# Reordering the first DMAs, table loads and a silu at the start of a 32-batch mixture-of-experts kernel

## The chip, the cores and the metric

The kernel runs on one core of a Trainium2 chip (trn2). The metric is the device time of one execution in microseconds. Beside it stands one profiled execution, whose trace gives every instruction on the engines TensorE (PE; its weight loads are PEld), VectorE (DVE), ScalarE (ACT), GpSimd (POOL) and SyncE (SP), and the packets of the DMA queues.

## The reference

The input x is 32 batches of 128 tokens by 128 features, fp32; cond is 32 by 128. Two layers follow each other, each "x plus a feed-forward of a conditioned mixture of experts". Only the front of the first layer matters here:

```
x = x + _L0_ffn_ref(_L0_cond_ref(x, cond_1024, ...), ...)
x = x + _L1_ffn_ref(_L1_cond_ref(x, cond_1024, ...), ...)

# in _L0_cond_ref
gate_logits = concat(means of three token groups) @ gate_w + gate_b
mod = silu(time_cond) @ time_w + time_b              # silu of cond
gate_logits = gate_logits * (1 + scale) + shift      # scale, shift: halves of mod
top 2 of softmax(gate_logits) weigh 4 experts per batch
out    = sum over experts of weight * mask * (gelu(x @ ew1 + eb1) @ ew2 + eb2)
shared = gelu(x @ sw1 + sb1) @ sw2 + sb2             # all tokens
return out + shared
```

Gelu is the tanh approximation. Inputs and weights are read from HBM by DMA.

## The kernel before, in words

Features lie on the 128 partitions and tokens along the free axis. The 4096 tokens are cut into 8 blocks of 512 (4 batches each): xT[0] to xT[7]. The first layer's shared expert works block by block. `shared_up` (L274 on) issues four matmuls (L279) of a block against the four 128-column chunks of `sw1_t`, each into a PSUM bank of its own, and for each a gelu on ScalarE with a bias from `par` (L280) into `hs`. `shared_down` (L286 on) adds the four second matmuls (L290, weights `sw2_t`) into one bank; VectorE writes the result to `c0all` (L294). In the profile the weights sw1_t and sw2_t are both called sw_t.

Blocks 0 to 4 are done first, then the routed experts: 36 units of one expert and up to two batches each, for which SP fetches weights by an index that the kernel computes itself; then blocks 5 to 7; then the feed-forward that takes most of the time (L253, L750), and the second layer. The function `pipelined` (L217) runs each unit's up part ahead of the previous unit's down part. So TensorE's order at the front is up 0, up 1, down 0, up 2, down 1, up 3, down 2 and so on. Matmul results take PSUM banks in rotation: six banks for `mm_tile`, two for `y_tile`; a matmul into a bank that was used before waits until its earlier reader is done.

Into this stream a table `between` (L639) hooks other work at named points, such as `("up", "s", 2, 2)`, in front of block 2's third up matmul: `cond_gates` (L301). It contains three small matmuls for the gate logits (L310), one of silu(cond) with time_w (L314), one of cond with the second layer's router weights (L316, read by VectorE into `tsb` at L317, which L433 multiplies into `diag`), and then a chain on VectorE with one exp on ScalarE (L327), giving the gate weights `gl` and the chosen experts `maskc`. `schedule` follows in front of block 3 (its small matmuls L356 and L357 need `maskc`), and `spread_slots` in front of block 4.

The order of instructions on each engine is made by the framework's scheduler from data dependences, except where `tc.keep_in_program_order(...)` pins an instruction to its place in the program. A scalar activation whose function isn't in the table that is loaded gets an ACT_TABLE_LOAD in front of it. Before the change nothing at the front is pinned on ScalarE: its silu of cond (L229), gelus and exp lie where the scheduler put them.

The first DMAs are issued on two queues, SP's and ScalarE's (L154 to L177):

```
    nc.scalar.dma_start(out=sw1_t[:, :P], in_=sw1[:, :P])         # L156
    nc.sync.dma_start(out=xT[0][:, half], in_=x[0][:, half])      # L157
    half = slice(TB // 2, TB)
    nc.scalar.dma_start(out=xT[0][:, half], in_=x[0][:, half])    # L159
    nc.sync.dma_start(out=sw1_t[:, rest_w], in_=sw1[:, rest_w])   # L160
    nc.scalar.dma_start(out=par, in_=packed)                      # L161
```

Sizes: 64 KB (L156), 128 KB each half of x[0], 192 KB (L160), and `par`, 411 columns of small parameters on 128 partitions, 205 KB. The first four columns of `par` are the shared expert's first biases, sb1. After these SP issues x[1] (L162), sw2 (L163), x[2] to x[7] (L165) and the big weights. Completions are counted on eight semaphores in rotation, so a DMA's issue can wait for the one that used its semaphore before.

`tiny` is a 1x1 tile that the second layer uses to ask for a table ahead of time (`table`, L877 on).

Of the kernel before, what the change touches and what calls it, by code (L numbers as in the profile page):

```python
# [34 lines left out]
AF = mybir.ActivationFunctionType  # L35
# [6 lines left out]
TB = BB * S  # L42
# [41 lines left out]
def columns(cols):  # L84
    out, at = {}, 0
    for name, n in cols:
        out[name] = slice(at, at + n)
        at += n
    return out, at


AT, NCOLS = columns(COLS)
# [6 lines left out]
def adaln_ffn(  # L99
# [3 lines left out]
    nc = tc.nc  # L103
# [14 lines left out]
    def mm_tile(name):  # L118
        taken["mm"] += 1
        return banks[:, (taken["mm"] - 1) % NM, :]  # L120
# [13 lines left out]
    def const(shape, name, dtype=F32):  # L134
        return cpool.tile(shape, dtype, tag=name, name=name)


    par = const([P, NCOLS], "par")
    par32 = const([P, NCOLS32], "par32")
    rows = const([P, NROW], "rows")  # L140
    sw1_t = wpool.tile([P, H], F32, tag="sw1", name="sw1_t")
# [8 lines left out]
    xT = [xall[:, b * TB : (b + 1) * TB] for b in range(NB)]  # L150
# [4 lines left out]
    half, rest_w = slice(0, TB // 2), slice(P, H)  # L155
    nc.scalar.dma_start(out=sw1_t[:, :P], in_=sw1[:, :P])  # L156
    nc.sync.dma_start(out=xT[0][:, half], in_=x[0][:, half])  # L157
    half = slice(TB // 2, TB)
    nc.scalar.dma_start(out=xT[0][:, half], in_=x[0][:, half])  # L159
    nc.sync.dma_start(out=sw1_t[:, rest_w], in_=sw1[:, rest_w])  # L160
    nc.scalar.dma_start(out=par, in_=packed)  # L161
    nc.sync.dma_start(out=xT[1], in_=x[1])  # L162
    nc.sync.dma_start(out=sw2_t, in_=sw2.rearrange("(c p) d -> p c d", p=P))  # L163
    for blk in range(2, NB):
# [14 lines left out]
    def col(name, i=0, n=1):  # L179
        return par[:, AT[name].start + i : AT[name].start + i + n]  # L180


    ones = const([B, P], "ones")
    nc.gpsimd.memset(ones, 1.0)
    tri = const([P, E1, E1], "tri")
    nc.gpsimd.memset(tri, 0.0)
    for e in range(1, E1):
# [38 lines left out]

    cT = par[:, AT["cond"]]
    sT = const([P, B], "sT")
    nc.scalar.activation(sT, cT, AF.Silu)  # L229
    full, hp, wp, head, prop, wrist = (const([P, B], n) for n in ("full", "hp", "wp", "hd", "pr", "wr"))  # L230

    def sums(blk):
        xb = batches(xT[blk])
        at = slice(blk * BB, (blk + 1) * BB)
        lo = 0
        for to, n in ((head, NHEAD), (prop, NPROP), (wrist, NHEAD)):
            V.tensor_reduce(to[:, at], xb[:, :, lo : lo + n], AX.X, ALU.add)
            lo += n
# [5 lines left out]
    def before(*point):  # L244
        for do in between.pop(point, ()):
            do()
# [27 lines left out]
    def shared_up(blk):  # L274
        h = work.tile([P, NC, TB], F32, tag="h", name=f"hs0_{blk}", bufs=3)
        ps = [mm_tile(f"us_{blk}_{c}") for c in range(NC)]
        for c in range(NC):
            before("up", "s", blk, c)
            nc.tensor.matmul(ps[c], lhsT=sw1_t[:, c * P : (c + 1) * P], rhs=xT[blk], start=True, stop=True)  # L279
            nc.scalar.activation(h[:, c, :], ps[c], AF.Gelu_apprx_tanh, bias=col("sb1", c))  # L280
        if blk < 2:
            for b in range(4 * blk, 4 * blk + 4):
                sums(b)
        return h
# [350 lines left out]
    def first_rows():  # L635
        gates_to_dram("f", 0)
        fgates[0] = fetch_rows(0)

    between.update({  # L639
        ("up", "s", 2, 2): [cond_gates],  # L640
        ("up", "s", 3, 0): [schedule],
        ("up", "s", 4, 0): [spread_slots],
# [8 lines left out]
    nc.gpsimd.memset(c0all[:, FIRST * TB :], 0.0)  # L651
    nc.gpsimd.memset(xall[:, NB * TB :], 0.0)
    L0 = {"s": (shared_up, shared_down), "p": (unit_up, unit_down)}
    units = [("s", b) for b in range(FIRST)] + [("p", q) for q in UNITS]
    units += [("s", b) for b in range(FIRST, NB)]
# [214 lines left out]
    def in_order(inst):  # L870


        tc.keep_in_program_order(inst)

    tiny = const([1, 1], "tiny")

    def table(func):  # L877

# [18 lines left out]
    def sh_up(group, k, of=None, h=None, later=None):  # L897

        e, c = divmod(k, 2)
        if h is None:  # L900
            h = work.tile([P, SB, TB], F32, tag="h", name=f"hs_{group}_{k}", bufs=3)
        for at, b in enumerate(blocks(group)):
            if of in (None, at):
                g, u = mm_tile(f"g1_{b}_{k}"), mm_tile(f"u1_{b}_{k}")
                by_columns(g, sws_t[0][:, e, c, :], x1T[b], 32)
                by_columns(u, sws_t[1][:, e, c, :], x1T[b], 32)


                def finish(g=g, u=u, at=at, b=b):
                    table(AF.Silu)  # L910
                    in_order(glu(g, u, h[:, at, :], f"s1_{b}_{k}"))

                finish() if later is None else later.append(finish)
        return h
# [162 lines left out]
    h = STAGES["f"][0](*units[0][1:])  # L1077
    for unit, after in zip(units, units[1:]):
# [3 lines left out]
        h = ahead  # L1082
# [4 lines left out]
    for group in (1, 2):  # L1087
# [49 lines left out]
        if group == 1:  # L1137
            h = sh_up(2, 0)
# [123 lines left out]
```

## Time and profile before

| what | value |
|---|---|
| time, median of 3 runs | 966.85 us (966.79 to 967.62) |
| the profiled execution: time, span | 966.89 us, 965.1 us |
| TensorE clock in the records (mean) | 1.00 |
| first matmul (L279), ended by the DMA of x | 4.54 us |
| silu of cond (L229), ended by the DMA of par | 7.38 us |
| first gelu (L280) | 8.92 us, 0.69 us long |
| tables loaded on ScalarE up to 24 us | 4, of 1.28 us each |
| exp of the gate (L327) | 22.27 us |
| first matmul of a routed expert (L521) | 41.73 us |
| DMA share and rate, 2.0 to 4.5 us | 0.92, 255 GB/s |

The span runs from the first to the last instruction; the profiled execution's own time is 1.8 us longer. In the timeline a row merges equal instructions that follow each other: start, length, engine, line, operation, written tile <- read tiles, partitions x elements, count, and in brackets the idle time before it and what ended it. An fp32 matmul call is two MATMUL rows (two passes), each with a weight load. A matmul's end is modelled and overlaps the next one's start, so the rate is read from starts.

### The profile page before, as it was taken

The numbers are of one execution on the slowest core, as the hardware profiler recorded it, in microseconds if no ns is written. First come the engines' busy times: TensorE is split into PE (matmuls) and PEld (weight loads), VectorE is DVE, ScalarE is ACT, GpSimd is POOL, SyncE is SP. The second block draws the span as 40 slices with busy tenths as digits, with TensorE's granted clock in tenths as the row PEclk, the third lists the DMA queues.
The fourth block names the chain that finished last, engine by engine and source line by source line (L and its number), as shares of the span: only waits on it lengthen the run. The fifth ranks groups of instructions, "written<-read, shape, count | busy, mean of one in ns | idle before, by whom it ended". The sixth has DMA issues, their size and how long they took to land.

```text
span 965.1 us, 15705 instructions
## 1 busy us (share of the span) xinstructions
PE 951.8 (99%) x6138; PEld 444.3 (46%) x6138; DVE 593.5 (61%) x1118; ACT 351.7 (36%) x622; POOL 75.1 (8%) x86
## 2 busy tenths in 40 slices
PE   8999999999999999999999999999999999999997
PEld 3588984444444444444444444444444443322333
DVE  4444574766866776686676887668667655633323
ACT  5355544223322322232232332223223223456674
POOL 0000001200101011010101011011010000000000
PEclk9999999999999999999999999999999999999999
DMA  9745641000000000000000000000000003040101
GB/s 315 245 143 171 213 138 48 2 1 4 1 1 2 1 1 1 1 1 1 2 2 1 1 2 3 1 2 1 1 1 1 1 1 89 1 91 1 45 2 45
DMA packets 22850, 38.13 MB, mean 40 GB/s; under 512 B 1968, under 2 KB 13232, under 8 KB 22768
## 3 DMA queue, kind: packets, MB, share of 16 engines
q1 hardware_dynamic: 22192, 36.48, 12.4%
q8 instruction: 53, 0.87, 0.4%
q10 hardware_dynamic: 576, 0.54, 0.2%
q14 instruction: 29, 0.24, 0.1%
HBM read 34.65 MB, written 2.36 MB: 38 GB/s over the span
## 4 chain that ended last, share of the span: by engine, by line
PE 84%; ACT 1%; DVE 0%; issue 0%; DVEq 0%; ACTq 0%
PE banks L253 57%; PE banks L750 20%; PE banks L890 3%; PE banks L290 1%; PE banks L984 1%; ACT hl L992 0%; PE banks L279 0%; PE banks L553 0%; PE banks L266 0%; PE banks L568 0%; PE banks L582 0%; DVE pg L978 0%; DVE pT L979 0%; ACT hs L280 0%; DVE fin L1176 0%
## 5 line engine op out<-in xcount | busy, mean ns | idle before, releaser
L667 ACT ACTIVATE sf<-banks 128x512 f32<-128x512 f32 x256 | 152.7, 597 | 435.3 <-PE banks L253 421.4
L668 DVE TENSOR_TENSOR hf<-sf,banks 128x512 f32<-128x512 f32 x256 | 174.8, 686 | 183.0 <-PE banks L253 182.2
L253 PE MATMUL banks<-c0all,wg_t 128*64 128x512 f32 x1024 | 263.5, 593 | 0.0
L253 PE MATMUL banks<-cg,wu_t 128*64 128x512 f32 x1024 | 263.1, 592 | 0.0
L253 PEld LDWEIGHTS banks<-cg,wu_t 128*64 128x64 f32 x1024 | 73.4, 137 | 146.3 <-issue 126.9
L253 PEld LDWEIGHTS banks<-c0all,wg_t 128*64 128x64 f32 x1024 | 72.8, 137 | 121.4 <-issue 108.8
L662 POOL PARTITION_BROADCAST fg<-fgT x64 | 72.7, 1149 | 655.1 <-DVE cg L711 493.6
L750 PE MATMUL banks<-t,wd_t 128*64 128x256 f32 x512 | 121.0, 379 | 0.0
L750 PE MATMUL banks<-hf,wd_t 128*64 128x256 f32 x512 | 104.2, 379 | 0.0
L750 PEld LDWEIGHTS banks<-hf,wd_t 128*64 128x64 f32 x512 | 53.4, 137 | 55.4 <-issue 36.8
L750 PEld LDWEIGHTS banks<-t,wd_t 128*64 128x64 f32 x512 | 70.1, 137 | 0.0
L524 ACT ACTIVATE h<-banks,w 128x256 f32<-128x256 f32 (+3 forms) x136 | 49.6, 433 | 49.4 <-PE banks L521 49.3
L750 PE MATMUL banks<-hf,a_sum 128*64 128x256 f32 x512 | 66.1, 379 | 0.0
L750 PE MATMUL banks<-t,a_sum 128*64 128x256 f32 x256 | 65.7, 379 | 0.0
L730 DVE TENSOR_TENSOR hf<-hf 128x512 f32<-128x512 f32 x64 | 63.0, 984 | 2.2
L253 PE MATMUL banks<-xall,rw_t 128*32 128x512 f32 x512 | 58.4, 593 | 0.2 <-ACT hl L992 0.2
L253 PE MATMUL banks<-xall,sws 128*32 128x512 f32 x512 | 57.4, 593 | 0.2 <-ACT hl L992 0.2
L537 PE MATMUL banks<-h,w 128*128 128x256 f32 (+3 forms) x272 | 52.5, 338 | 0.0
L521 PE MATMUL banks<-x,w 128*128 128x256 f32 (+3 forms) x272 | 52.2, 337 | 0.0
L521 PEld LDWEIGHTS banks<-x,w 128*128 128x128 f32 x272 | 45.3, 190 | 4.4 <-issue 1.0
L537 PEld LDWEIGHTS banks<-h,w 128*128 128x128 f32 x272 | 44.7, 190 | 4.1 <-issue 0.7
L965 ACT ACTIVATE hr<-banks 128x512 f32<-128x512 f32 x64 | 36.9, 591 | 25.6 <-PE banks L253 25.4
(211 smaller groups left out, 775.1 us busy)
## 6 DMA issues: line engine op xcount, KB each, us to landing
w<-in_experts SPq DMA_DIRECT2D x36, 514.5 KB
wg_t<-in_w_gate SPq DMA_DIRECT2D x8, 256.0 KB
wu_t<-in_w_up SPq DMA_DIRECT2D x8, 256.0 KB
wd_t<-in_w_down SPq DMA_DIRECT2D x8, 256.0 KB
gates<-rg SPq DMA_DIRECT2D x4, 512.0 KB
gates<-rg SPq DMA_DIRECT2D x8, 256.0 KB
xall<-in_x SPq DMA_DIRECT2D x7, 256.0 KB
out<-fin SPq DMA_DIRECT2D x6, 256.0 KB
```

Source lines behind the costliest of these rows:

```text
L253: mm = nc.tensor.matmul(ps[own, :], lhsT=w[:, own], rhs=x, start=True, stop=True)
L290: nc.tensor.matmul(y, lhsT=sw2_t[:, c, :], rhs=h[:, c, :], start=(c == 0), stop=(c == NC - 1))
L521: nc.tensor.matmul(ps[c][:, :m, :n], lhsT=w1, rhs=x[:, :m, :n], start=True, stop=True)
L524: nc.scalar.activation(h[:, c, :m, :n], ps[c][:, :m, :n], AF.Gelu_apprx_tanh, bias=bias)
L537: nc.tensor.matmul(y[:, :m, :n], lhsT=w2, rhs=h[:, c, :m, :n], start=(c == 0), stop=(c == NC - 1))
L662: nc.gpsimd.partition_broadcast(bc, row)
L667: silu = nc.scalar.activation(s, ps_gate, AF.Silu)
L668: V.tensor_tensor(h, s, ps_up, ALU.mult)
L730: V.tensor_tensor(b12, b12, b11, ALU.subtract)
L750: nc.tensor.matmul(y[half, n], lhsT=w[:, c, :], rhs=h[:, c, :], start=first, stop=(e == EF - 1 and last))
L890: in_order(nc.tensor.matmul(y[32 * j : 32 * (j + 1)], lhsT=w, rhs=h, start=first, stop=last))
L965: in_order(nc.scalar.activation(h[:, at, :], ps, AF.Gelu))
```

## The change

It does four things at the front. The DMA of the small parameters is split: the four bias columns go second on ScalarE's queue, the other 407 columns fourth. The second half of x[0] goes on SP's queue instead of ScalarE's, and the rest of sw1 on ScalarE's instead of SP's. A 1x1 gelu on `tiny` (allocated earlier, behind `ones`) stands in front of all other activations and is pinned, as are the gelus of blocks 0 and 1. And the silu of cond is hooked in front of the first matmul of down 0, which by the program's order is behind block 1's gelus, and pinned there.

```diff
     half, rest_w = slice(0, TB // 2), slice(P, H)
     nc.scalar.dma_start(out=sw1_t[:, :P], in_=sw1[:, :P])
     nc.sync.dma_start(out=xT[0][:, half], in_=x[0][:, half])
-    half = slice(TB // 2, TB)
-    nc.scalar.dma_start(out=xT[0][:, half], in_=x[0][:, half])
-    nc.sync.dma_start(out=sw1_t[:, rest_w], in_=sw1[:, rest_w])
-    nc.scalar.dma_start(out=par, in_=packed)
+    half, biases = slice(TB // 2, TB), AT["sb1"].stop
+    nc.scalar.dma_start(out=par[:, :biases], in_=packed[:, :biases])
+    nc.sync.dma_start(out=xT[0][:, half], in_=x[0][:, half])
+    nc.scalar.dma_start(out=sw1_t[:, rest_w], in_=sw1[:, rest_w])
+    nc.scalar.dma_start(out=par[:, biases:], in_=packed[:, biases:])
     nc.sync.dma_start(out=xT[1], in_=x[1])
...
     nc.gpsimd.memset(ones, 1.0)
+
+    tiny = const([1, 1], "tiny")
+    tc.keep_in_program_order(nc.scalar.activation(tiny, ones[:1, :1], AF.Gelu_apprx_tanh))
...
     sT = const([P, B], "sT")
-    nc.scalar.activation(sT, cT, AF.Silu)
...
-            nc.scalar.activation(h[:, c, :], ps[c], AF.Gelu_apprx_tanh, bias=col("sb1", c))
+            gelu = nc.scalar.activation(h[:, c, :], ps[c], AF.Gelu_apprx_tanh, bias=col("sb1", c))
+            if blk < 2:
+                tc.keep_in_program_order(gelu)
...
     between.update({
+        ("down", "s", 0, 0): [lambda: tc.keep_in_program_order(nc.scalar.activation(sT, cT, AF.Silu))],
         ("up", "s", 2, 2): [cond_gates],
...
-
-    tiny = const([1, 1], "tiny")
```

The built program after the change, engine by engine, has ScalarE do: gelu table, 1x1 gelu, 8 gelus, silu table, silu, gelu table, 2 gelus of block 2, exp table, exp, gelu table, 2 gelus of block 2, then as before. Before: silu table, silu, gelu table, 11 gelus, exp table, exp, gelu table, 1 gelu. On TensorE the matmul of L316 moves behind block 2's third and fourth up matmuls, and of block 4's four down matmuls one instead of two stands in front of the first routed unit. On VectorE the copy of `tsb` and the product `diag` move behind the subtraction that feeds exp (L326). SP has the same number of DMAs, the third x block's now with a wait for an earlier DMA.

## The prediction

> **What bounds the kernel now.** I read the page first, then the timeline of TensorE and of its weight loads from 0 to 46 us, then ScalarE's over the same stretch, then the DMA queues of the microseconds before the first matmul. The page:
>
> ```profile
> span 965.1 us, 15705 instructions
> ...
> PE 951.8 (99%) x6138; PEld 444.3 (46%) x6138; DVE 593.5 (61%) x1118; ACT 351.7 (36%) x622; POOL 75.1 (8%) x86
> ```
>
> TensorE's share is 99%, but a busy PE need not be a PE at its peak, so the start is looked at closely. Its timeline (start, length, engine, line, operation, operands, count; each fp32 matmul call is two passes):
>
> ```profile
> 4.54 9.07 PE L279 MATMUL banks<-xall,sw_t 128*128 128x512 f32 x16 [4.54 <-DMA xall<-in_x]
> 13.45 3.60 PE L290 MATMUL banks<-hs,sw_t 128*128 128x512 f32 x8
> 16.89 1.88 PE L279 MATMUL banks<-xall,sw_t 128*128 128x512 f32 x4
> 18.70 0.23 PE L310 MATMUL banks<-par,full 128*32 128x4 f32 x2
> ...
> 18.91 0.21 PE L314 MATMUL banks<-par,sT 128*32 128x8 f32 x2
> 18.97 0.21 PE L316 MATMUL banks<-par 128*32 128x8 f32 x2
> 19.11 1.98 PE L279 MATMUL banks<-xall,sw_t 128*128 128x512 f32 x4
> 20.93 3.60 PE L290 MATMUL banks<-hs,sw_t 128*128 128x512 f32 x8
> ```
>
> The reader is to see that the only idle time is the 4.54 us in front, and that a DMA of the input x ends it. From then on each row begins where the one before lets it: 8 passes in 3.44 us (13.45 to 16.89) is 0.429 us a pass, and the same 0.429 holds whether gelus are late or early. Up to 136 us TensorE has no idle gap. The weight loads show the rate of the first passes:
>
> ```profile
> 5.53 0.34 PEld L279 LDWEIGHTS banks<-xall,sw_t 128*128 128x128 f32 x1 [0.52 <-issue]
> 6.38 0.34 PEld L279 LDWEIGHTS banks<-xall,sw_t 128*128 128x128 f32 x1 [0.52 <-issue]
> 7.23 0.34 PEld L279 LDWEIGHTS banks<-xall,sw_t 128*128 128x128 f32 x1 [0.52 <-issue]
> 8.09 0.34 PEld L279 LDWEIGHTS banks<-xall,sw_t 128*128 128x128 f32 x1 [0.52 <-issue]
> 8.73 0.19 PEld L279 LDWEIGHTS banks<-xall,sw_t 128*128 128x128 f32 x1 [0.31 <-issue]
> 9.16 0.19 PEld L279 LDWEIGHTS banks<-xall,sw_t 128*128 128x128 f32 x1 [0.24 <-issue]
> ```
>
> They come 0.85 us apart until 8.09 and 0.43 apart from 8.73: TensorE runs at half rate for some 4 us (to about 8.5), though the clock row says 1.00. ScalarE:
>
> ```profile
> 2.13 1.28 ACT L229 ACT_TABLE_LOAD   x1 [2.13 <-issue]
> 7.38 0.23 ACT L229 ACTIVATE sT<-par 128x32 f32<-128x32 f32 x1 [3.97 <-DMA par<-in_packed]
> 7.63 1.28 ACT L280 ACT_TABLE_LOAD   x1
> 8.92 3.70 ACT L280 ACTIVATE hs<-banks,par 128x512 f32<-128x512 f32 x6
> ...
> 17.94 0.69 ACT L280 ACTIVATE hs<-banks,par 128x512 f32<-128x512 f32 x1 [3.60 <-PE banks L279]
> ...
> 20.98 1.28 ACT L327 ACT_TABLE_LOAD   x1
> 22.27 0.20 ACT L327 ACTIVATE gl<-gl 32x4 f32<-32x4 f32 x1
> 22.49 1.28 ACT L280 ACT_TABLE_LOAD   x1
> ```
>
> The first gelu starts at 8.92, although its matmul ended near 6.6: ScalarE waited for all of par (silu at 7.38), then loaded gelu's table. That looks like 2.3 us to win, but nobody waits for them. The first matmul that needs a bank back is call 7, at 11.73; it wants the first gelu, over at 9.61: 2.1 us to spare. The second GEMM starts at 13.45, when block 0's four gelus have been over since 11.3. ScalarE then idles 3.60 us before 17.94. So in this stage TensorE's own issue sets the end, behind the arrival of its first operands.
>
> **The change, part by part.** *Gelu's table first, biases in a DMA of their own.* ScalarE now issues four DMAs at 0.45 us each (0.73 to 2.55), loads the table (to 3.85), and does the 1x1 activation. Its first gelu can start when call 1 ends. Gain on the path: 0, since TensorE fills the 2.1 us of slack already; the gelus just wait for matmuls. The biases are 128 rows of 16 B; the trace's 80-byte packets (rows) take 12 ns, so they cost some 0.1 us of an engine's time and should land by about 3.5, against a need near 5.8. If they came 2 us later, that slack would still cover them.
>
> *Order of the first DMAs.* This is the part that lies on the path, because the start of TensorE is set by the second half of x[0]. Before, that half went second on ScalarE's queue, beside the 192 KB rest of sw1 on SP's. The packets of the trace: the second half 2.81 to 4.04, its completion 4.40; the sw1 rest 2.54 to 3.88, its completion 4.22; first matmul 4.54. The queues from 2.5 to 4.05 us (packets, MB, share of 16 engines):
>
> ```profile
> q1 hardware_dynamic: 207, 0.27, 62.9%
> q10 hardware_dynamic: 235, 0.18, 41.2%
> ```
>
> Both queues are served side by side, SP's (q1) getting more bytes. After the change the half of x goes second on SP's queue and takes the place that the sw1 rest had there (packets from 2.54); beside it run the tail of sw1's first quarter, the biases, and only then the sw1 rest, third on ScalarE's queue, issued 0.46 us later than before. Upper bound of the gain: the half alone, 0.13 MB at the 0.29 MB/us of this window, ends at 2.54 + 0.45 = 2.99, so 1.05 us sooner; sw1's first quarter, whose completion came at 3.29, limits that to 1.1 as well. Lower bound: 0, if the sw1 rest takes the same share as before. Nearest row: the sw1 rest itself in that place, 192 KB against a competitor, in 1.34 us; 128 KB at its rate is 0.89 us, which ends at 3.43, 0.6 sooner; since its competitor is nearly empty at first I take 0.65. First matmul at 3.9.
>
> Does the sw1 rest become late? It is wanted two passes later, 3.9 + 1.84 = 5.74. Nearest row: its own transfer before, 1.68 us from first packet to completion; from about 2.9 that gives 4.6. The other end: third on ScalarE's queue before was par, of the same size, 3.69 to 7.36; that span from 2.9 gives 6.6 and a stall of 0.8. I take 4.6, since the traffic beside it is the x half and x[1], not par's neighbour with its many 512-byte packets. Cost 0.
>
> x[1] and sw2 keep their places in SP's queue (wanted at 9.4 and 12.8, completed at 7.18 and 7.89). The third block's DMA, which went out at 2.58, now waits for the first quarter of sw1 (3.3); two 256 KB transfers stand queued ahead of it, so nothing runs dry. What SP issues behind it is unchanged, and w of the first pair landed at 37.3, used at 41.7.
>
> *Silu behind the second block's gelus.* It now costs two table loads more on ScalarE there (silu, and gelu again), and the stage has five loads instead of four. They stand in order before block 2's gelus, the exp and block 3's. From the rows: the last gelu of block 1 ends at 14.34; 1.28 + 0.23 + 1.28 and some 0.05 between give 17.2, and the next gelu's matmul is ready at 17.94. Covered by the 3.60 us of idle time, 0.75 left; without cover it would cost up to 2.8. The Trainium skill speaks against this step: "ScalarE: Activation LUTs", section "What ACT_TABLE_LOAD costs", charges every switch a drain beside the load, about 2.66 us in all, and its rules say to batch by table set. With it silu would last until 19.9, and the exp likewise (below). The trace shows 1.28 us, next instruction 0.01 to 0.02 us later: exp's excursion takes 20.96 to 23.79, which is 2 x 1.28 + 0.20 + 0.06. The row decides; cost 0.
>
> *What the scheduler moved with it.* The built order differs in three places. Exp is now asked for after two of block 2's gelus instead of three: table by 20.8, its input (VectorE's chain, without the tsb copy and diag product) by 20.4, so it runs 1.5 us earlier, and the last two gelus end at 23.6 instead of 24.5. The tsb copy now stands in front of the softmax sum and waits for its matmul, about 21.2; the sum still comes 0.7 us sooner than its 22.51. And the matmul of L316 (cond by r1t) leaves the group of five small ones and stands alone behind block 2's last up matmul. Small matmuls have a fixed price per group: five take 18.17 to 19.64 where two large passes would take 0.86, so 0.61; two (L356, L357) take 23.93 to 25.20, so 0.41. That is 0.07 a call and 0.28 a group. One group more: +0.27, on the path. The later regrouping of block 4's second GEMM around the first expert pair moves no total.
>
> Sum: -0.65 + 0.27 = -0.38. The profiled execution took 966.89 (1.8 around its span); the median shown is 966.85. So 966.5.
>
> **The rivals.**
> *Nothing gained in front.* The sw1 rest takes its share all the same and the start stays at 4.54: 966.85 + 0.27 = 967.1. Or the start moves but the half rate ends at the same instant, 8.5. The Trainium skill, "TensorE: Matmul & The Clock Gate", Part 1, has the gate judge a free-running window, so the half-rate stretch need not begin with the kernel. The trace shows one such stretch, 4.0 us. If it moves along, 0.65 counts in full; if it ends where it ended, 0.33: 966.8. Being free-running, on average over launches it counts in full, which is what I use. For this rival: both queues share the engines, so what one gains the other takes. Against it: the x half gets a place in which packets began at 2.54 instead of 2.81, and meets less beside it.
>
> *Slower: the second piece of weights is late.* Third on ScalarE's queue, the sw1 rest lands at 6.6 as par's row would have it. From 5.74 on TensorE stands still, 0.8 us, and the quiet pushes the end of half rate back by a window (3.4 us in the same section of the skill, half of it lost, 1.7). -0.38 + 0.8 + 1.7 = +2.1: 969.0. It decides from a landing after about 5.7. Against it: the piece's own 1.68 us.
>
> *The drain is real on a switch from silu.* First gelu of block 2 at 19.9, exp over at 24.0, its mask at 25.8 where L356 would want it at 24.7 (stall 1.05), and bank 4 free at 27.4 where block 3's second matmul comes at 26.95 (0.45): 966.5 + 1.5 = 968.0.
>
> *Half rate shorter.* The window falls well and half rate ends one half to one window sooner than its 4 us: a further 0.9 to 1.7, so 964.8 to 965.6.
>
> **How the numbers follow.** Forecast 0.58 (966.5, its own range 966.0 to 967.0); nothing gained 0.22 (966.8 to 967.1); late weights 0.07 (969.0); drain 0.05 (968.0); shorter half rate 0.08. The range 965.6 to 967.9 covers the first two and takes in the three shown runs' spread of 0.8; it leaves out late weights and nearly all of the last two, 0.2 at most. About 0.2%, 1.9 us, is what a measurement of this kernel can tell from no change: faster (under 964.9) is most of the last case, 0.05; slower (over 968.8) is late weights, 0.07; the rest 0.88.
>
> **What would show it.** In the changed profile: the first L279 matmul near 3.9 instead of 4.54; weight loads 0.85 apart for about 4 us, no gap between the second and third; first gelu near 5.8 instead of 8.92; silu's excursion inside 14 to 17.3 with a wait for TensorE before the next gelu; a lone small matmul with about 0.28 around it near 21; everything after 25 us shifted by one constant, about -0.4. I am wrong if TensorE shows an idle gap between its second pass and 25 us, if the start stays above 4.3, or if the shift is not constant after 46 us.

## The result and the profile after

The changed kernel takes 969.1 us (median of 22 runs, 967.95 to 969.95), beside 967.37 us for the kernel before in 22 runs (966.28 to 968.33). The ratio is 1.0017, 95% interval 1.0011 to 1.0023: slower by about 1.7 us. The forecast of 966.5 and its range up to 967.9 missed it. The time is close to that of the rival with the late second piece of weights (969.0), in part by luck: the rival was worked out as +2.1 from a before of 966.85, the median of three runs, where 22 runs give 967.37 and a shift of +1.7. The profiled execution took 969.95, its span is 968.2. It is one of the slowest of its 22, and the profile before (966.89) is 0.5 under its median, so the shift between the two profiles (+3.1) is larger than that of the medians (+1.7).

The page after, as before (busy time, share, instructions):

```profile
span 968.2 us, 15710 instructions
...
PE 954.4 (99%) x6138; PEld 445.2 (46%) x6138; DVE 593.5 (61%) x1118; ACT 353.7 (37%) x624; POOL 75.1 (8%) x86
```

TensorE has the same 6138 instructions and still 99%, and is busy 2.6 us longer. So most of what the profile lost hides inside "busy". The timeline of TensorE at the front (line numbers are three to five higher than before: L282 is the up matmul, L295 the down matmul, L321 the lone small one):

```profile
3.76 2.04 PE L282 MATMUL banks<-xall,sw_t 128*128 128x512 f32 x2 [3.76 <-DMA xall<-in_x]
7.12 9.11 PE L282 MATMUL banks<-xall,sw_t 128*128 128x512 f32 x14 [1.31 <-DMA sw_t<-in_sw]
16.07 3.60 PE L295 MATMUL banks<-hs,sw_t 128*128 128x512 f32 x8
19.50 1.88 PE L282 MATMUL banks<-xall,sw_t 128*128 128x512 f32 x4
...
21.66 1.98 PE L282 MATMUL banks<-xall,sw_t 128*128 128x512 f32 x4
23.57 0.23 PE L321 MATMUL banks<-par 128*32 128x8 f32 x2
23.73 3.70 PE L295 MATMUL banks<-hs,sw_t 128*128 128x512 f32 x8
```

The start came 0.78 us sooner (3.76 for 4.54). But the row of 16 passes is cut behind the second: 1.31 us of idle time, ended by a DMA of sw_t, the rest of sw1. By the distance of 1.84 us between the first and third passes of before, the third was due at 5.60; it came 1.52 later (more than the idle time, as the end of a pass is modelled). The weight loads show the second loss:

```profile
3.73 0.50 PEld L282 LDWEIGHTS banks<-xall,sw_t 128*128 128x128 f32 x2 [3.73 <-DMA sw_t<-in_sw]
7.12 0.50 PEld L282 LDWEIGHTS banks<-xall,sw_t 128*128 128x128 f32 x2 [2.88 <-DMA sw_t<-in_sw]
8.13 0.34 PEld L282 LDWEIGHTS banks<-xall,sw_t 128*128 128x128 f32 x1 [0.52 <-issue]
...
12.40 0.34 PEld L282 LDWEIGHTS banks<-xall,sw_t 128*128 128x128 f32 x1 [0.52 <-issue]
13.06 0.19 PEld L282 LDWEIGHTS banks<-xall,sw_t 128*128 128x128 f32 x1 [0.33 <-issue]
13.49 0.19 PEld L282 LDWEIGHTS banks<-xall,sw_t 128*128 128x128 f32 x1 [0.24 <-issue]
```

Loads stay 0.85 us apart until 12.40, where before they were 0.43 apart from 8.73. The trace's record of the granted clock says the same: full from 8.51 before, from 12.86 after. Laid against the passes of before, the shift is -0.78 at the start, +0.74 at the third pass, +2.6 at the tenth, +2.9 behind the lone L321, and +3.1 at the end. In this execution: -0.78 (start) + 1.52 (stall) + 1.87 (longer half rate) + 0.30 (L321) = +2.91. From 46 us on the shift is not quite the one constant that was forecast: it stays at 2.91 to 118 us, grows there by 0.16 and at 167 us by 0.04, and then stays at 3.11. What adds these 0.2 is open.

ScalarE went as forecast, moved along by TensorE's delay:

```profile
2.61 1.28 ACT L188 ACT_TABLE_LOAD   x1 [2.61 <-issue]
3.90 0.20 ACT L188 ACTIVATE tiny<-ones 1x1 f32<-1x1 f32 x1
5.84 0.69 ACT L283 ACTIVATE hs<-banks,par 128x512 f32<-128x512 f32 x1 [1.74 <-PE banks L282]
...
16.97 1.28 ACT L645 ACT_TABLE_LOAD   x1
18.27 0.23 ACT L645 ACTIVATE sT<-par 128x32 f32<-128x32 f32 x1
18.51 1.28 ACT L283 ACT_TABLE_LOAD   x1
20.56 0.69 ACT L283 ACTIVATE hs<-banks,par 128x512 f32<-128x512 f32 x1 [0.76 <-PE banks L282]
```

The first gelu starts 3.08 us sooner than before, and behind the silu's two loads ScalarE still idles 0.76 us until its matmul is there.

Where the piece of weights was: the queues from 3.25 to 4.25 us, SP's (q1) and ScalarE's (q10), as packets, MB and share of the 16 engines. Of before:

```profile
q1 hardware_dynamic: 98, 0.14, 58.5%
q10 hardware_dynamic: 133, 0.13, 52.3%
```

Of after:

```profile
q1 hardware_dynamic: 46, 0.09, 53.9%
q10 hardware_dynamic: 61, 0.06, 17.4%
```

The engines moved 0.15 MB there instead of 0.27. The rest of sw1 had its first packet at 3.25 and completed at 7.07; x[1], third on SP's queue, completed at 6.89. Before, the two second-place transfers had completed at 4.22 and 4.40, and the third-place ones at 7.18 (x[1]) and 7.36 (par).

### The profile page after: what moved, and what is told of

It reads as the page before. It is cut to its first block, busy times and chain, and to the rows that moved or that the text cites. A ratio compares the mean times of both kernels' runs of the same rounds, so it can differ in the third digit from the quotient of the medians.

```text
span 968.2 us, 15710 instructions
## 1 busy us (share of the span) xinstructions
PE 954.4 (99%) x6138; PEld 445.2 (46%) x6138; DVE 593.5 (61%) x1118; ACT 353.7 (37%) x624; POOL 75.1 (8%) x86
## 4 chain that ended last, share of the span: by engine, by line
PE 83%; ACT 1%; DVE 0%; issue 0%; DVEq 0%; ACTq 0%
PE banks L256 57%; PE banks L756 20%; PE banks L894 3%; PE banks L295 1%; PE banks L988 1%; ACT hl L996 0%; PE banks L282 0%; PE banks L558 0%; PE banks L269 0%; PE banks L573 0%; PE banks L587 0%; DVE pg L982 0%; DVE pT L983 0%; ACT hs L283 0%; DVE fin L1180 0%
```

## The experiments

The theory (late by its place): what goes third on ScalarE's queue shares the engines with x[1], third on SP's, and lands near 7 as par did before; TensorE stops behind its second pass, and the stop prolongs the half rate. The rivals: the loss is elsewhere, in the silu with its two table loads or in the small matmul ("elsewhere"); the stop counts with its length only, and doesn't prolong the half rate ("stop alone"); and later, the 16-byte rows of the biases clog the queues ("small rows"). Ratios are to the kernel before on the same chip, with 95% intervals. The cuts of the edits show the lines that are new; of the lines that they replace, some are left out.

**One part alone.** Into the kernel before goes only the order of the DMAs (e4), and into it only the swap of the two second transfers, without the biases (e1):

```diff
 # e4_dma_part: before, with
+    half, biases = slice(TB // 2, TB), AT["sb1"].stop
+    nc.scalar.dma_start(out=par[:, :biases], in_=packed[:, :biases])
+    nc.sync.dma_start(out=xT[0][:, half], in_=x[0][:, half])
+    nc.scalar.dma_start(out=sw1_t[:, rest_w], in_=sw1[:, rest_w])
+    nc.scalar.dma_start(out=par[:, biases:], in_=packed[:, biases:])
 # e1_swap_only: before, with
+    nc.sync.dma_start(out=xT[0][:, half], in_=x[0][:, half])
+    nc.scalar.dma_start(out=sw1_t[:, rest_w], in_=sw1[:, rest_w])
+    nc.scalar.dma_start(out=par, in_=packed)
```

> The kernel before with the DMA part of the change alone (biases second, rest of sw1 third, other parameters fourth on ScalarE's queue; x half second on SP's); silu and the tables where they were before. Late-weights theory: start near 3.8, a gap of about 1.3 us before the third pass, half rate until one window later in most runs: the whole loss less the lone small matmul, 969.1 - 0.3 = 968.8. Rival, ScalarE's order: back to 967.4 or below.

> The kernel before, with one exchange: the second half of x[0] second on SP's queue, the rest of sw1 second on ScalarE's; par whole and third, silu and tables as before. Late-weights theory (what hurts is the third place on ScalarE's queue): here the rest of sw1 is second and runs beside the x half, lands by about 4.4, TensorE starts at about 4.2 and has no gap before its third pass; time 967.4 - 0.3 = 967.1. Rival, the queue itself (ScalarE's queue loses against SP's wherever the piece stands): the piece lands after 5.9, a gap of about 1 us as in the changed kernel, time near 969. Rival, ScalarE's new order: no difference to before at all, 967.4.

e4: 968.69 us, 1.0015 (1.0008 to 1.0021). The order of the DMAs alone makes nearly the whole loss. What is missing (0.2 us by the two ratios, less than their intervals can tell) fits the 0.3 of the lone small matmul, which e4 doesn't have. "Elsewhere" falls. Its TensorE:

```profile
3.79 2.04 PE L280 MATMUL banks<-xall,sw_t 128*128 128x512 f32 x2 [3.79 <-DMA xall<-in_x]
6.88 2.93 PE L280 MATMUL banks<-xall,sw_t 128*128 128x512 f32 x3 [1.05 <-DMA sw_t<-in_sw]
```

The same early start and nearly the same stop, with silu and gelus where they were. e1: 966.9 us, 0.9998 (0.9989 to 1.0006). With the piece second on ScalarE's queue it lands at 4.39 and there is no stop; the start is 4.29, 0.25 sooner (TensorE up to 9 us):

```profile
4.29 5.46 PE L279 MATMUL banks<-xall,sw_t 128*128 128x512 f32 x6 [4.29 <-DMA xall<-in_x]
```

The swap of the two queues is harmless; what hurts is that the biases stand in front of the piece.

**The change with the piece in time.** Both are the changed kernel with the biases third on ScalarE's queue: e3 with the piece second there and the x half on SP's queue, e2 with both on the queues of before.

```diff
 # e3_biases_third: after, with
-    nc.scalar.dma_start(out=par[:, :biases], in_=packed[:, :biases])
     nc.sync.dma_start(out=xT[0][:, half], in_=x[0][:, half])
     nc.scalar.dma_start(out=sw1_t[:, rest_w], in_=sw1[:, rest_w])
+    nc.scalar.dma_start(out=par[:, :biases], in_=packed[:, :biases])
 # e2_old_places: after, with
+    nc.scalar.dma_start(out=xT[0][:, half], in_=x[0][:, half])
+    nc.sync.dma_start(out=sw1_t[:, rest_w], in_=sw1[:, rest_w])
+    nc.scalar.dma_start(out=par[:, :biases], in_=packed[:, :biases])
```

> The changed kernel with two DMAs of ScalarE's queue exchanged: the rest of sw1 second, the biases third. Late-weights theory: start near 4.2, rest of sw1 landed by 4.5, no gap, 967.4 - 0.3 + 0.3 = 967.4; the first gelu is not later than its matmul, since biases land by about 5. Rival, the queue itself: the gap of about 1.3 us stays, 969. Rival, the small DMA: the gap stays, since the 16-byte rows are still there.

> The changed kernel, with the second half of x[0] and the rest of sw1 on the queues of before; the biases third on ScalarE's queue, the other parameters fourth; gelu table first and silu moved as in the change. Late-weights theory: start at 4.5, no gap behind the second pass, half rate over about 4 us after the start, and what is left of the change is one small matmul that stands alone, +0.3: 967.7. Rival, ScalarE's order (silu and its two table loads cost TensorE something): stays near 969. Rival, the small DMA of 16-byte rows: a stall remains too, at least 968.5.

e3: 966.97 us, 0.9999 (0.9991 to 1.0008); start 4.08, no stop (up to 9 us):

```profile
4.08 5.42 PE L282 MATMUL banks<-xall,sw_t 128*128 128x512 f32 x6 [4.08 <-DMA xall<-in_x]
```

e3 and the changed kernel differ only in the order of the piece and the biases, and their intervals do not meet: this exchange alone takes the loss away. e2: 967.71 us, 1.0004 (0.9995 to 1.0012); start 4.45, no stop. In e2 everything of the change but the order of the DMAs is left. Its lone small matmul stands between large ones:

```profile
19.71 1.99 PE L282 MATMUL banks<-xall,sw_t 128*128 128x512 f32 x4
21.63 0.23 PE L321 MATMUL banks<-par 128*32 128x8 f32 x2
21.79 3.70 PE L295 MATMUL banks<-hs,sw_t 128*128 128x512 f32 x8
```

From 19.71 to 21.79 is 2.08 us for four large passes and the small call, against the 1.72 of four passes at 0.43; what the small call would have cost inside its group, 0.07, leaves 0.29. The shift against before grows by 0.29 at this place in e2 and by 0.30 in e3. In these traces it is the only price that the silu, the gelus and the scheduler's moves put on the path; the time of e2 fits it, but its interval holds no change as well.

**The stop filled.** The first up matmul is done twice (the second writes the same values), so that TensorE has work where it stood still:

```diff
 # e5_filled: after, with
+            for _ in range(2 if blk == 0 and c == 0 else 1):
                 nc.tensor.matmul(ps[c], lhsT=sw1_t[:, c * P : (c + 1) * P], rhs=xT[blk], start=True, stop=True)
```

> The changed kernel, in which TensorE does the very first matmul call twice (the same result into the same bank), so that it works through most of its gap. Theory with two terms (the gap of 1.3 us, and the half rate that lasts longer because TensorE stood still): the second call takes 1.7 us at half rate, the third pass pair starts 0.3 us later than in the changed kernel, but half rate ends at the first boundary after some 4 to 7 us of work instead of starting its count again after the gap: in the trace half rate over by about 10.5 at the latest; time 0.5 to 1.0 us below the changed kernel's 969.1, so 968.3. Rival, only waiting costs and the half-rate stretch is what it is: 969.4, slower than the changed kernel by the 0.3.

967.88 us, 1.0008 (1.0000 to 1.0016). "Stop alone" wanted 969.4, slower than the changed kernel, which is a ratio of 1.0021 and lies outside this interval, so it falls: the idle time itself prolonged the half rate. With two passes more to do, the kernel came out 0.9 us faster than the changed one (1.0017) by the ratios; the two intervals overlap, so the size is not settled. In this trace the x half landed late and TensorE started late with it:

```profile
4.82 10.21 PE L283 MATMUL banks<-xall,sw_t 128*128 128x512 f32 x18 [4.82 <-DMA xall<-in_x]
```

So its stages can't be laid beside those of after, and that the second call fills the stop from an early start is not shown in a trace; the time of its runs is the evidence.

**Other places for the piece.** In e6 sw2 goes in front of x[1] on SP's queue, in e8 the piece goes fourth on ScalarE's, behind the other parameters:

```diff
 # e6_sw2_beside: after, with
+    nc.sync.dma_start(out=sw2_t, in_=sw2.rearrange("(c p) d -> p c d", p=P))
     nc.sync.dma_start(out=xT[1], in_=x[1])
-    nc.sync.dma_start(out=sw2_t, in_=sw2.rearrange("(c p) d -> p c d", p=P))
 # e8_fourth: after, with
+    nc.scalar.dma_start(out=par[:, biases:], in_=packed[:, biases:])
     nc.scalar.dma_start(out=sw1_t[:, rest_w], in_=sw1[:, rest_w])
-    nc.scalar.dma_start(out=par[:, biases:], in_=packed[:, biases:])
```

> The changed kernel with two DMAs of SP's queue exchanged: sw2 (four 512-byte rows a partition) third, x[1] fourth. If queues are served packet by packet in turn, the rest of sw1 (1536-byte packets, third on ScalarE's queue) now gets three quarters of the engines instead of four tenths and lands near 4.7: no gap, time as e3, 967.2. If it is the third place itself (what both queues have in flight goes slowly at 3.3 to 4.3 us whatever it is), it lands at 6 or later and the gap stays near 1 us: 968.8.

> The changed kernel with the suspected cost made larger: the rest of sw1 fourth on ScalarE's queue, behind the other parameters. Late-weights theory: it lands near 8.0, the gap behind the second pass grows from 1.3 to about 2.3 us, time 969.1 + 1.0 to 1.3 = 970.2. Rival, the gap is no cost of its own (something later absorbs it): stays at 969.1.

e6: 967.72 us, 1.0007 (0.9999 to 1.0016), between the two numbers that were expected; the piece landed at 5.43, and the third pass was in time. That trace is the second fastest of its 12 runs (966.65), so most of the others were probably less lucky. From first packet to completion the piece took 1.74 us here. With x[1] beside it, what stood third on ScalarE's queue (192 or 205 KB) took 2.8 to 3.8 us in the traces of before, e1, e7, after, e4 and e9. So what lies on the other queue counts: 512-byte rows of sw2 in place of x[1]'s 2048-byte rows brought the piece in 1.64 us sooner than in after. e8: 969.19 us, 1.0023 (1.0014 to 1.0031), less than the 970.2 that was expected, and not told apart from the changed kernel:

```profile
3.76 2.05 PE L282 MATMUL banks<-xall,sw_t 128*128 128x512 f32 x2 [3.76 <-DMA xall<-in_x]
7.49 8.37 PE L282 MATMUL banks<-xall,sw_t 128*128 128x512 f32 x14 [1.68 <-DMA sw_t<-in_sw]
```

Fourth place means a landing at 7.45, only 0.4 behind third place: as the third and fourth transfers overlap, one place costs little there, while from second to third it cost 2.7 (4.39 in e1, 7.07 in after).

**Small rows or place.** In e9 the second transfer on ScalarE's queue has 128 columns of par in place of 4, so rows of 512 bytes. In e10 sw1 comes in pieces, in the order in which TensorE wants them, and the biases behind:

```diff
 # e9_wide_biases: after, with
-    half, biases = slice(TB // 2, TB), AT["sb1"].stop
+    half, biases = slice(TB // 2, TB), P
 # e10_rest_in_two: after, with
-    nc.scalar.dma_start(out=par[:, :biases], in_=packed[:, :biases])
     nc.sync.dma_start(out=xT[0][:, half], in_=x[0][:, half])
-    nc.scalar.dma_start(out=sw1_t[:, rest_w], in_=sw1[:, rest_w])
+    nc.scalar.dma_start(out=sw1_t[:, P : 2 * P], in_=sw1[:, P : 2 * P])
+    nc.scalar.dma_start(out=sw1_t[:, 2 * P :], in_=sw1[:, 2 * P :])
+    nc.scalar.dma_start(out=par[:, :biases], in_=packed[:, :biases])
```

> After, but the piece of par that goes second on ScalarE's queue is 128 columns wide instead of 4: 128 rows of 512 bytes, 64 KB, in place of 128 rows of 16 bytes. Theory A, small rows: in every kernel so far with the 16-byte rows second, both queues moved only 83 to 152 GB/s from 3.25 to 4.25 us, against 272 to 379 elsewhere. If the 16-byte rows do that, the rate there is back above 270, the rest of sw1 lands near 5, the gap before the third pass is gone: 967.5. Theory B, place: whatever goes third on ScalarE's queue starts when SP's queue starts x[1] and shares with it, and the slow stretch comes from both starting together. Then the rest of sw1 still lands at 6.5 to 7.5, the gap before the third pass is 1 us or more, and the time is 969 to 970, as after.

> After, but ScalarE's queue carries sw1 in pieces in the order in which TensorE wants them and the biases behind them: columns 0 to 127 first, 128 to 255 second (64 KB), 256 to 511 third (128 KB), biases fourth, the other parameters fifth. Theory (late by place): the second piece lands before 4.5, so the third pass is on time; the third piece is wanted at the start plus four passes at half rate, 3.4 us behind the start, about 7.3, and lands between 5.5 and 7: no gap, or one below 0.3 us, and 967.0 to 967.6. If a third place is late whatever stands in front (landing after 7.3), a gap of up to 1 us stands before the fifth pass instead and the time is 968.3 or more. The biases in fourth place land by 8; if they land after about 7.5, the first gelu holds the fifth and later calls' banks no longer than to 9, which TensorE wants at about 10.8: no cost.

e9: 968.77 us, 1.0016 (1.0009 to 1.0023). The piece landed at 6.55:

```profile
3.69 2.05 PE L282 MATMUL banks<-xall,sw_t 128*128 128x512 f32 x2 [3.69 <-DMA xall<-in_x]
6.60 8.36 PE L282 MATMUL banks<-xall,sw_t 128*128 128x512 f32 x14 [0.86 <-DMA sw_t<-in_sw]
```

"Small rows" falls (theory A in this expectation): with wide rows the queues moved 136 GB/s from 3.25 to 4.25 us, where theory A wanted over 270, and the stop is there. It is a little shorter, 0.86 where at least 1 was expected, and the time, just under the 969 to 970 of theory B, is that of the changed kernel within the intervals. e10: 966.58 us, 0.9992 (0.9986 to 0.9999), faster than the 967.0 to 967.6 that was expected and, barely clear of no change, than before. TensorE has no gap, and its half rate ends early:

```profile
3.90 8.99 PE L283 MATMUL banks<-xall,sw_t 128*128 128x512 f32 x16 [3.90 <-DMA xall<-in_x]
12.73 3.60 PE L296 MATMUL banks<-hs,sw_t 128*128 128x512 f32 x8
```

The start is 0.64 sooner than before; behind the lone small matmul the shift against before is -0.43: this is the forecast's sum (-0.65 + 0.27) in a kernel that keeps the weights in time. Its second piece landed at 3.93, the third at 5.94, wanted at 7.3. The biases came fourth:

```profile
3.87 1.28 ACT L189 ACT_TABLE_LOAD   x1 [3.87 <-DMA sw_t<-in_sw]
5.17 0.20 ACT L189 ACTIVATE tiny<-ones 1x1 f32<-1x1 f32 x1
6.55 0.69 ACT L284 ACTIVATE hs<-banks,par 128x512 f32<-128x512 f32 x1 [1.18 <-DMA par<-in_packed]
```

Gelu's table even waits for the issue of the fifth DMA on ScalarE, and the first gelu for the biases, 0.71 later than in after; it costs nothing, as the forecast said of the gelus' slack.

**What the start still holds.** e7 is e1 with the first matmul call cut into two of 256 columns, so that the first needs only the first half of x[0]:

```diff
 # e7_first_in_halves: e1, with
+            for at in ((slice(0, TB // 2), slice(TB // 2, TB)) if blk == 0 and c == 0 else (slice(0, TB),)):
+                nc.tensor.matmul(ps[c][:, at], lhsT=sw1_t[:, c * P : (c + 1) * P], rhs=xT[blk][:, at], start=True, stop=True)
```

> A version meant to be faster than both: the kernel before with the exchange of e1 (x half second on SP's queue, rest of sw1 second on ScalarE's), and the first matmul call cut into two of 256 columns, of which the first needs one half of x[0] only. Theory (TensorE's start is what counts, its work goes on at once): start at about 3.45 instead of 4.54, no gap longer than 0.2 behind it, half rate moves along on average: 967.0 - 1.0 = 966.0. Rival (half rate ends where it would have ended, only half of the earlier start counts): 966.5. Rival (the second half of x comes late and the gain is a wait in another place): 967.0.

966.17 us, 0.9987 (0.9979 to 0.9995): the lowest median of all, faster than both kernels; e10's interval overlaps with its own.

```profile
3.30 9.29 PE L280 MATMUL banks<-xall,sw_t 128*128 128x256 f32 x18 [3.30 <-DMA sw_t<-in_sw]
12.42 3.60 PE L291 MATMUL banks<-hs,sw_t 128*128 128x512 f32 x8
```

It starts at 3.30, now held by the first quarter of sw1, and needs neither the early table nor the moved silu.

**The half rate across all of them.** From each trace: the first matmul, the instant of full clock, and the distance.

| kernel | start | full clock from | distance | stop (idle) |
|---|---|---|---|---|
| before | 4.54 | 8.51 | 4.0 | 0 |
| e1 / e2 / e3 | 4.29 / 4.45 / 4.08 | 9.74 / 9.95 / 9.34 | 5.5 / 5.5 / 5.3 | 0 |
| e5 / e6 / e7 / e10 | 4.82 / 3.90 / 3.30 / 3.90 | 9.36 / 8.24 / 7.67 / 7.71 | 4.5 / 4.3 / 4.4 / 3.8 | 0 |
| after | 3.76 | 12.86 | 9.1 | 1.31 |
| e4 | 3.79 | 13.09 | 9.3 | 1.05 |
| e8 | 3.76 | 11.74 | 8.0 | 1.68 |
| e9 | 3.69 | 10.83 | 7.1 | 0.86 |

Without a stop the distance is 3.8 to 5.5 us; with a stop of 0.9 to 1.7 us in it, 7.1 to 9.3. The four with a stop average 8.4, of which 1.2 is the stop, so 7.2 us at half rate against 4.7 for the eight without: 2.5 us more, half of it lost, 1.2 us. That is one trace each, and those of after and e4 are among the slowest of their runs. e8 and e9, whose traces are nearer to the middle of theirs, have 6.3 us without the stop: 1.6 more, 0.8 lost. The stage where the stretch ends varies, which may be why the runs of one kernel spread over some 2 us.

## Why the prediction was wrong

**The step that failed** is the answer to "Does the sw1 rest become late?": "I take 4.6, since the traffic beside it is the x half and x[1], not par's neighbour with its many 512-byte packets. Cost 0." It landed at 7.07, and TensorE stood still: its third pass came 1.52 us late. I had two rows, the piece's own 1.68 us in second place and par's 3.69 to 7.36 in third place, and took that of the same data. The row of the same place was the right one: par's 3.67 us there, the piece's 3.82 (3.25 to 7.07; the first packet came 0.35 later than the 2.9 that I put). The reason that I gave does not hold. Par had the same neighbours in the trace of before: x[1] on SP's queue with its first packet at 3.54, and 512-byte rows of sw2 only from 5.11 on (in after: 3.12 and 4.72). And of the two x[1] is the worse one: with the 512-byte rows in its place the piece came at 5.43 (e6, one trace).

**The rival's size.** It put 0.8 us on the stall and 1.7 on the half rate, together 2.5. In the profiled execution they are 1.52 and 1.87. For the medians take e3, which differs from after only in the order of the piece and the biases: 969.1 - 966.97 is 2.1 (1.7 by the two ratios), and after starts 0.32 sooner, so the late weights cost 2.0 to 2.4. If the stall in these runs is that of the trace, 1.52, that leaves 0.5 to 0.9 for the half rate, an estimate that only after's one trace supports. Then the sum was nearly right by luck, since its two terms were off in opposite directions. What the Trainium skill gives in "TensorE: Matmul & The Clock Gate", Part 1, a free-running window of 3.4 us, is the step in which the stretch can grow. The traces agree with the window: the clock's records have it full for 955.732 us before and for 952.319 after, 3.413 apart, and these are 280 and 279 times 3.4133. That a stop of this length costs such a step in some executions and not in others is argued, not shown. By the estimate above, 0.5 to 0.9 us is 1.0 to 1.8 us of stretch at half rate, so on average a third to a half of a window was added, where I had put a whole one.

**The chance.** I gave this case 0.07. The wrong row decided that, too: as par's row was at least as near as the piece's own, it should have stood near a half. That the stop is worth more than its length was in the rival's sum; only the chance was too low.

**The rest of the sum held.** Start: 3.9 forecast, 3.76 in after (0.65 of gain forecast, 0.78 found). Lone small matmul: 0.27 forecast, 0.30 found, 0.29 in e2. The first gelu near 5.8: 5.84. Nobody waits for the gelus: in e10 they come later still and TensorE doesn't stop. Silu behind the second block's gelus: 1.28 us a load. The first ends at 18.25 and silu starts at 18.27; the second ends at 19.79, and the next gelu starts at 20.56, when its matmul is there. So there is none of the drain of about 1.4 us that the Trainium skill charges ("ScalarE: Activation LUTs", section "What ACT_TABLE_LOAD costs"); the row was right to decide, and the drain's rival falls. "Nothing gained in front" falls as well: the place does bring the start forward (e10, 966.58). "Half rate shorter" did not happen in after: from its start to the full clock it took 9.1 us, the stop included, instead of 4.0.

## What to carry to other kernels

When a transfer is moved in a queue, estimate its landing from what stood in that place before, with the same neighbour on the other queue, and not from its own duration elsewhere; then check the second piece of data as closely as the first. An early start that runs dry can be worse than a later one without a gap: here 0.78 us won in front was followed by a stall of 1.5 us and a longer stretch at half rate. Order the first transfers by when the engine that bounds the kernel wants them; small parameters that only a slack engine waits for go behind.

## What the runs showed of the hardware

**A slow stretch of the queues.** Where the second transfers hold little data, so that their last packets end by 3.6 us (3.3 in after; in e5 one engine's end at 4.4), the third transfers are then nearly alone on both queues, and the engines move little while they are busy for half to four fifths of the time. In before, e1, e2, e3 and e7 the second transfers end at 3.9 to 4.1. The window 3.25 to 4.25 (length, then busy time and count of PE, PEld, DVE, ACT and POOL, clock, share and GB/s) in after:

```profile
3.25:4.25 1.00, 0.49 (x1) 0.50 (x2) 0.53 (x3) 0.84 (x2) 0.00 (x0) 1.00 0.71 152
```

In e3, and in e10:

```profile
3.25:4.25 1.00, 0.17 (x1) 0.20 (x2) 0.20 (x1) 0.85 (x2) 0.00 (x0) 1.00 1.08 379
```

```profile
3.25:4.25 1.00, 0.35 (x1) 0.38 (x2) 0.39 (x2) 0.38 (x1) 0.00 (x0) 1.00 0.81 162
```

It is 83 to 162 GB/s in after, e4, e5, e6, e8, e9 and e10, and 272 to 379 in before, e1, e2, e3 and e7. It ends between 4.0 and 4.5 in all of them, and before and e7 have a short one as well, from 3.75 to 4.25. The width of the rows doesn't make it (e9), nor does x[1] on the other queue (e6, with sw2 there, has the stretch too). Nor is it needed for a late third place: in e1, which doesn't have it, par still took 3.21 us (3.71 to 6.92). Why the engines are slow there stays open. In e10 it does no harm, since the piece wanted next had passed ahead of it.

**The clock column and the half rate.** The windows give the clock as 1.00 throughout the stretch in which weight loads come at half their rate (0.85 us apart in after up to 12.40). The distance between the loads shows that stretch, and the clock's own records show its end (12.86); the column shows neither.
